# Which channels of a Haar inverse put their last convolution off: 27 instead of 23 of 64, two and three apart

## The chip, the cores and the metric

The kernel runs on one core of one Trainium2 chip. The metric is the device time of one execution in microseconds (us). Before the change the median of three runs is 2845.51 us (2843.74 to 2846.02). The engines are named as in the profile: PE (TensorE: matmul), DVE (VectorE), ACT (ScalarE), POOL (GpSimd) and SP (SyncE, which here only issues transfers).

## What is computed

The input x is 4 batches of 64 channels of 256 x 256, in float32. Four layers follow each other. Layers 0, 1 and 3 are separable long convolutions: each channel is convolved with the outer product of two filters, and gets a bias times itself added. Layer 2 is a Haar transform in two dimensions, then a mixing over the channels of each coefficient, and the inverse transform with x added:

```python
def _conv(x, ...):                       # layers 0, 1, 3, shortened
    k = einsum('ijk,imk->ijmk', hx, hy)  # one outer product per channel
    y = irfft2(rfft2(x, 2L) * rfft2(k, 2L))[..., :L, :L]
    return y + x * bias[:, None, None]

def _haar(x, v, conv_w, tau):            # layer 2
    f1 = haar2d(x)
    acc = 0
    for i in range(2):
        f4 = einsum('bchw,oc->bohw', f1 * v[i], conv_w[i])
        acc = acc + sign(f4) * relu(abs(f4) - tau[i])
    return haar2d(acc, inverse=True) + x
```

The convolutions of one channel don't depend on other channels; the mixing needs all 64 channels of a batch, and so does each channel of the inverse.

## The kernel before, in words

**A convolution** is two products with Toeplitz matrices of the two filters (`contract`, L283: four matmuls each, lines L286 and L287, each of which the profile shows twice[...]). The first product `pa` is copied out of PSUM by ACT (L300), the second, `py`, takes that copy, and DVE adds the bias term while it reads `py` from PSUM (L317). The Toeplitz tile `t` of a channel is loaded from a padded filter in HBM (L277, 256 KB, six buffers).

**The stages.** For each batch: `convolutions` (layers 0 and 1, and the Haar transform of the columns), `mixing` (64 groups of coefficients), `inverse` (64 channels). The convolutions of batch b + 1 are spread over the mixing of batch b, with a few at the edges. In the mixing, a group is loaded (`f`, L460), mixed by PE into `px` (L480), scaled partly by DVE (L502) and partly by ACT (L507, 8 columns in the last batch, 12 in the others), then ACT takes the size and the sign (L511, L514), and DVE subtracts the threshold, puts the sign back, and adds (L518, L522, L528). In the inverse of a channel, ACT gathers the coefficients (`zc`, L569), PE does the rows (`pw`, L576 and L577, called row matmuls below), the first 16 channels also need a column matmul (`pu`, L590), DVE joins the result with the saved part `r` (loaded at L558; L598, L601, L602) into `u`. Further halvings of columns (L326, L329) run on DVE during the first 38 channels. Then layer 3 follows for the channel: `pa`, its copy, `py`, its sum, and the store to the output from ACT's queue.

**Put-off channels.** In the inverses of batches 0 to 2 the channels in the list `put_off` (L673) do not run layer 3. Their `u` is stored to the HBM buffer `late` from SP's queue (`aside`, L606), their Toeplitz tile isn't loaded (`sooner`, L561). The last mixing has no convolutions of a next batch beside it; there `convolution` (L655) loads `u` back as the tile `v` (L662, three buffers), and the Toeplitz tile, runs layer 3 and stores to the output from SP's queue (L652).

**The order of the work.** Time is counted in ticks: one mixing group or one inverse channel is one tick. The table `PLACE` gives each step a place in ticks relative to its channel's or group's tick (for a put-off channel in the last mixing: load at +0.316, `pa` and its copy at +1.855, `py` and its sum at +2.783, store at +4.4). All steps are collected as events, sorted by that place (L723) and emitted in this order; the scheduling layer that records the program then sets the final order on each engine. Each engine works in order. `spread` (L669) lays n convolutions over a number of ticks, rounded down to whole ticks: the put-off ones over the 71 ticks from two before the last mixing to three before its inverse. In an inverse, a channel that is not put off is shifted a little within its tick (L644) unless both neighbours are put off: one pair of shifts for a channel that follows a put-off one, the other for a channel that stands before one.

Of the kernel before, what the change touches and what calls it, by code (L numbers as in the profile page):

```python
# [16 lines left out]
B, C, S, EMB, ORD = 4, 64, 256, 33, 64  # L17
# [93 lines left out]
def conv_seq_kernel(ctx, tc, x, fz, fw, bias, decay, haar, haar_row, factors, vt, taut, wmix, out):  # L111
# [236 lines left out]
    def at(time, run, unit):  # L348
        events.append((time, len(events), run, unit))
# [201 lines left out]
    def inverse(b, start, put_off):  # L551
# [78 lines left out]
        for c in range(C):  # L630
            for name, stage in zip(("sooner", "early", "fetch", "rows"), (sooner, early, fetch, rows)):
                at(start + c + PLACE[name], stage, c)
            turn = start + c
            if c < 16:
                at(start + c + PLACE["halves"], halves, c)
                at(start + c + PLACE["cols"], cols, c)
                turn += 1
            at(turn + PLACE["join"], join, c)
            if c in put_off:
                at(turn + PLACE["aside"], aside, c)  # L640
            else:
                shift = (0.0, 0.0)
                if put_off and not {c - 1, c + 1}.issubset(put_off):
                    shift = ((-0.27, -0.342), (0.23, 0.158))[c % 3]  # L644
                for name, stage in zip(("a3", "a3 copy", "y3", "y3 sum", "out"), last(b, st)):
                    at(turn + PLACE[name] + shift[name[0] != "a"], stage, c)

    def last(b, st, queue=nc.scalar):
        return [
            *first(b, st, "u", 2, "a3"),  # L650
            *second(b, st, "a3", 2, "u", "y3", "co"),
            lambda c: queue.dma_start(out[b, c].rearrange("(k p) w -> p k w", p=P), st.pop(c)["y3"]),  # L652
        ]
# [16 lines left out]
        return [begin + i * (end - begin - 1) // (n - 1) for i in range(n)]  # L670


    put_off = [*range(2, 53, 3), *range(53, C, 2)]  # L673

    clamped = {}, {}, {}
    one = filters(0, nc.scalar, clamped[0], None, clamped[1])
# [33 lines left out]
    for b in range(B):  # L710
        mixing(b, start, N_ACT[b])
        end = start + groups + 3
        if b + 1 < B:
            ready = convolutions(b + 1, spread(ahead, end + 2), in_parts=range(C), border=end)
        else:
            convolution(
                [(i, c) for i in range(B - 1) for c in sorted(put_off)], spread(start - 2, end + 2, (B - 1) * len(put_off))
            )
        inverse(b, end, put_off if b + 1 < B else ())

        start = max(end + C, ready + 3)
        ahead = start - 3
# [114 lines left out]
```

## Time and profile before

The profiled execution took 2842.56 us; its span, from the first to the last instruction, is 2840.7 us. The granted clock is 1.00 throughout.

| what | us | share of the span |
|---|---|---|
| PE busy | 2732.7 | 96% |
| DVE busy | 2494.6 | 88% |
| ACT busy | 2077.6 | 73% |
| POOL busy | 333.9 | 12% |

The stages, from the first `px` or `pw` of one to that of the next:

| stage | from, us | length, us | DMA, GB/s |
|---|---|---|---|
| convolutions of batch 0 | 20 | 415 | 236 |
| mixing 0 and convolutions of batch 1 | 435.4 | 420.1 | 209 |
| inverse 0, with 41 convolutions of layer 3 | 855.5 | 184.5 | 274 |
| mixing 1 and convolutions of batch 2 | 1040.0 | 458.5 | 209 |
| inverse 1, with 41 convolutions | 1498.5 | 184.5 | 275 |
| mixing 2 and convolutions of batch 3 | 1683.0 | 458.5 | 210 |
| inverse 2, with 41 convolutions | 2141.5 | 179.8 | 277 |
| mixing 3, with 69 put-off convolutions | 2321.3 | 289.4 | 244 |
| inverse 3, with 64 convolutions | 2610.7 | 230 | 221 |

The list of transfers gives, from issue to landing, a median of 4.1 us for `t` and for `r`, 3.5 for `f`, and 4.2 for the stores to the output from ACT's queue.

How to read it: a share of busy time over the whole span mixes stages that different engines bound, so each stage has to be looked at by itself. Records of one engine overlap (the next instruction starts before the record of the last ends), so an instruction's cost on a full engine is the distance between starts, not the length of its record. Idle time counts only on the engine that bounds its stage.

### The profile page before, as it was taken

How to read it: one execution, taken by the hardware profiler on the slowest of the kernel's cores; microseconds unless marked ns; L12 is line 12 of the kernel's file. 1: busy time of each engine (PE TensorE's matmuls, PEld its weight loads, DVE VectorE, ACT ScalarE, POOL GpSimd, SP SyncE). 2: the span in 40 equal slices, each digit the busy share in tenths (PEclk: the TensorE clock that was granted, in tenths of full speed). 3: DMA queues.
4: the chain of work that ended last, by engine and by line, in shares of the span. 5: the costliest groups of instructions: out<-in, count | busy, mean ns of one | idle time of the engine just before them, and what ended most of it. 6: DMA issues, size and time to landing. Idle time of an engine off the chain costs nothing. (4 is left out here: it accounts for less than half of the span.)

```text
span 2840.7 us, 56683 instructions
## 1 busy us (share of the span) xinstructions
PE 2732.7 (96%) x18642; PEld 2438.6 (86%) x18642; DVE 2494.6 (88%) x4333; ACT 2077.6 (73%) x4941; POOL 333.9 (12%) x644
## 2 busy tenths in 40 slices
PE   9999999999999999999999999999999999899999
PEld 8999998888889898888889998888889987787998
DVE  5655558999998979999998879999998889999985
ACT  2333348999986559989886658999985669998554
POOL 0111111121111001212210001312210000000000
PEclk9999999999999999999999999999999999999999
DMA  6877787676667886777677986777778988787786
GB/s 200 258 232 231 227 239 220 209 208 208 206 207 251 287 257 203 211 212 209 205 216 246 292 262 201 210 210 214 208 212 241 296 277 249 234 253 228 227 240 200
DMA packets 597209, 653.20 MB, mean 230 GB/s; under 512 B 44625, under 2 KB 513204, under 8 KB 596660
## 3 DMA queue, kind: packets, MB, share of 16 engines
q1 hardware_dynamic: 545460, 599.82, 70.6%
q10 hardware_dynamic: 51456, 49.75, 5.1%
q8 instruction: 150, 2.46, 0.4%
q14 instruction: 143, 1.17, 0.1%
HBM read 428.34 MB, written 221.05 MB: 229 GB/s over the span
## 5 line engine op out<-in xcount | busy, mean ns | idle before, releaser
L286 PE MATMUL py<-t,a 128*128 128x256 f32 x3072 | 946.3, 390 | 48.7 <-ACT a L300 47.7
L300 ACT COPY a<-pa 128x512 f32<-128x512 f32 x768 | 475.1, 619 | 476.6 <-PE pa L287 448.3
L507 ACT ACTIVATE f<-px,vt 128x64 f32<-128x64 f32 x2816 | 607.6, 354 | 104.2 <-DVE f L502 101.9
L287 PEld LDWEIGHTS py<-t,a 128*128 128x128 f32 x3072 | 583.4, 190 | 79.3
L287 PE MATMUL py<-t,a 128*128 128x128 f32 x3072 | 590.0, 274 | 0.0
L286 PEld LDWEIGHTS py<-t,a 128*128 128x128 f32 x3072 | 479.4, 191 | 112.2 <-ACT a L300 74.6
L380 POOL TENSOR_TENSOR sd<-less 128x128 f32<-128x128 f32 (+4 forms) x320 | 188.5, 589 | 1829.7 <-DVE less L379 1498.1
L286 PE MATMUL pa<-t,y 128*128 128x256 f32 x1024 | 316.5, 391 | 45.0 <-DVE y L317 44.2
L569 ACT COPY zc<-z 128x512 f32<-128x512 f32 x256 | 280.8, 1105 | 104.6 <-PE pw L577 96.7
L518 DVE TENSOR_TENSOR mag<-mag,vt 128x1024 f32<-128x1024 f32 x256 | 316.5, 1236 | 7.5 <-ACT mag L511 6.7
L522 DVE SCALAR_TENSOR_TENSOR mag<-mag,f 128x1024 f32<-128x1024 f32 x256 | 317.4, 1240 | 0.9 <-ACT f L514 0.5
L286 PE MATMUL pa<-t,x 128*128 128x256 f32 x1024 | 308.7, 383 | 0.6 <-DMA pad<-z 0.6
L403 DVE TENSOR_TENSOR sp<-sd,sp 128x512 fp32r<-128x512 f32 x256 | 179.3, 700 | 145.7 <-ACT sp L398 144.3
L480 PE MATMUL px<-wb,f 64*128 64x128 f32 x4096 | 303.7, 285 | 2.2 <-ACT f L507 2.2
L511 ACT ACTIVATE mag<-f 128x1024 f32<-128x1024 f32 x256 | 293.9, 1148 | 5.2 <-DVE z L528 1.2
L514 ACT ACTIVATE f<-f 128x1024 f32<-128x1024 f32 x256 | 283.9, 1109 | 4.1
L480 PEld LDWEIGHTS px<-wb,f 64*128 64x128 f32 x4096 | 252.2, 187 | 36.5 <-ACT f L507 3.0
L317 DVE SCALAR_TENSOR_TENSOR y<-x,bsb,py 128x512 f32<-128x512 f32 x256 | 190.3, 743 | 44.0 <-PE py L287 40.6
L286 PE MATMUL pa<-t,u 128*128 128x256 f32 x748 | 224.6, 382 | 0.7 <-PE pw L577 0.7
L287 PEld LDWEIGHTS pa<-t,y 128*128 128x128 f32 x1024 | 194.5, 190 | 26.4
L287 PEld LDWEIGHTS pa<-t,x 128*128 128x128 f32 x1024 | 194.6, 190 | 26.3
L286 PEld LDWEIGHTS pa<-t,y 128*128 128x128 f32 x1024 | 155.6, 191 | 65.3 <-DVE y L317 62.8
(71 smaller groups left out, 4434.6 us busy)
## 6 DMA issues: line engine op xcount, KB each, us to landing
t<-pad SPq DMA_DIRECT2D x767, 256.0 KB, 4.1
x<-in_x SPq DMA_DIRECT2D x256, 256.0 KB, 3.9
coef<-co SPq DMA_DIRECT2D x256, 256.0 KB, 3.2
f<-coef SPq DMA_DIRECT2D x256, 256.0 KB, 3.5
r<-keep SPq DMA_DIRECT2D x256, 256.0 KB, 4.1
out_y<-y ACTq DMA_DIRECT2D x187, 256.0 KB, 4.2
keep<-sums SPq DMA_DIRECT2D x256, 128.0 KB, 2.8
keep<-sd SPq DMA_DIRECT2D x256, 128.0 KB, 2.7
```

The source lines that it names most:

```text
L286: nc.tensor.matmul(ps[:, m, :], src[:, 0, m * P : (m + 1) * P], t[:, ::-1], start=True, stop=False)
L287: nc.tensor.matmul(ps[:, m, P:], src[:, 1, m * P : (m + 1) * P], t[:, : P - 1 : -1], start=False, stop=True)
L300: nc.scalar.copy(a, s["p" + new])
L317: nc.vector.scalar_tensor_tensor(y, s[res], bsb[:, layer, c : c + 1], s["p" + new], ALU.mult, ALU.add)
L380: engine.tensor_tensor(t[:, :, :, half:length], v[..., 0], v[..., 1], ALU.subtract)
L480: nc.tensor.matmul(ps[:, r, q, h * P : (h + 1) * P], f[half, q, h * P : (h + 1) * P], wb[half], start=True, stop=True,)
L507: nc.scalar.mul(f4[:, j], px[:, j // 4 % 2, j // 8, j % 4], scale(g, 0)[:, j : j + 1])
L511: nc.scalar.activation(mag, st[g]["f4"], AF.Abs)
L514: nc.scalar.activation(st[g]["f4"], st[g]["f4"], AF.Sign)
L518: nc.vector.tensor_sub(mag, mag, over(g, 1, 16))
L522: nc.vector.scalar_tensor_tensor(mag, mag, 0.0, st[g]["f4"], ALU.max, ALU.mult)
L569: nc.scalar.copy(a, v)
```

## The change

The list of put-off channels gets 27 members in place of 23. Before, it was every third channel from 2 to 50 and every second from 53 to 63. After, it is 2, 5, 7, 10, 12, 15 and so on up to 45, two and three apart in turn, then every second channel from 47 to 63. The three inverses keep 37 convolutions each in place of 41, and the last mixing gets 81 in place of 69. Since 81 is more than 71, `spread` puts two of them into one tick at ten of the ticks (the first of these, -2, 5 and 12, counted from the start of the last mixing, then every seventh up to 61); before, two of the ticks had none. The pair of shifts is now chosen by whether the next channel is put off, where before it was chosen by the channel's number modulo 3.

```diff
                 if put_off and not {c - 1, c + 1}.issubset(put_off):
-                    shift = ((-0.27, -0.342), (0.23, 0.158))[c % 3]
+                    shift = ((-0.27, -0.342), (0.23, 0.158))[c + 1 in put_off]
...
-    put_off = [*range(2, 53, 3), *range(53, C, 2)]
+    put_off = [c for c in range(46) if c % 5 in (0, 2) and c] + [*range(47, C, 2)]
```

## The prediction, made before the changed kernel was run

> **What bounds the kernel now.** I first read the busy time by stage (from the busy windows), because the change moves work from three stages into a fourth. The columns are the window and its length, then busy time and instruction count of each engine, the granted clock, the DMA share and GB/s.
>
> ```profile
> core 0: us, PE busy (x) PEld busy (x) DVE busy (x) ACT busy (x) POOL busy (x), PEclk, DMA share, GB/s
> 855.00:1040.00 185.00, 183.29 (x1200) 167.93 (x1198) 160.33 (x308) 111.12 (x145) 6.83 (x19) 1.00 0.86 274
> 1498.00:1683.00 185.00, 183.40 (x1200) 168.40 (x1198) 152.73 (x296) 112.67 (x147) 5.45 (x20) 1.00 0.87 275
> 2141.00:2321.00 180.00, 178.40 (x1167) 163.57 (x1167) 150.65 (x292) 111.15 (x145) 5.45 (x20) 1.00 0.89 277
> 1624.40:1680.00 55.60, 55.58 (x380) 51.98 (x379) 43.39 (x85) 32.04 (x38) 0.00 (x0) 1.00 0.93 290
> 2321.00:2600.00 279.00, 254.48 (x2051) 221.43 (x2050) 275.25 (x462) 265.49 (x694) 0.00 (x0) 1.00 0.81 245
> ```
>
> The first three rows are the inverses of batches 0 to 2: PE has work 99% of the time, DVE 83 to 87%, ACT 60%. The fourth is the last 24 ticks of one of them, where DMA reaches 0.93. The last row is the last mixing with the put-off channels in it: there DVE is full (99%), ACT 95%, PE 91%. So a channel that is put off leaves a stage that PE bounds and enters one that DVE bounds.
>
> Then I read the order of time on DVE and PE. DVE, at the end of the last mixing (start, us, line):
>
> ```profile
> 2595.89 1.34 DVE L518 TENSOR_TENSOR mag<-mag,vt 128x1024 f32<-128x1024 f32 x1
> 2597.02 0.88 DVE L528 TENSOR_TENSOR z<-mag 128x256 f32<-128x256 f32 x2
> 2597.69 1.35 DVE L522 SCALAR_TENSOR_TENSOR mag<-mag,f 128x1024 f32<-128x1024 f32 x1
> 2598.82 0.87 DVE L317 SCALAR_TENSOR_TENSOR y<-v,bsb,py 128x512 f32<-128x512 f32 x1
> 2599.48 0.88 DVE L502 TENSOR_TENSOR f<-px,vt 128x256 f32<-128x256 f32 x2
> 2600.14 1.35 DVE L518 TENSOR_TENSOR mag<-mag,vt 128x1024 f32<-128x1024 f32 x1
> ```
>
> A tick is the time from one L518 to the next: 2600.14 - 2595.89 = 4.25 us, with no idle time. Records overlap, so what an instruction costs is its distance to the next start: the put-off channel's sum (L317) costs 2599.48 - 2598.82 = 0.66 us, the rest of the tick 3.6.
>
> PE inside an inverse:
>
> ```profile
> 1585.00 0.38 PE L287 MATMUL pa<-t,u 128*128 128x128 f32 x2
> 1585.22 0.27 PE L577 MATMUL pw<-hrow,zc 128*128 128x128 f32 x1
> 1585.33 0.39 PE L576 MATMUL pw<-hrow,zc 128*128 128x128 f32 x2
> 1585.55 0.27 PE L577 MATMUL pw<-hrow,zc 128*128 128x128 f32 x1
> 1585.66 0.39 PE L576 MATMUL pw<-hrow,zc 128*128 128x128 f32 x2
> 1586.06 0.70 PE L286 MATMUL py<-t,a 128*128 128x256 f32 x2
> ...
> 1594.86 0.60 PE L286 MATMUL py<-t,a 128*128 128x256 f32 x2
> 1595.29 0.38 PE L287 MATMUL py<-t,a 128*128 128x128 f32 x2
> 1595.51 0.60 PE L286 MATMUL py<-t,a 128*128 128x256 f32 x2
> 1595.95 0.38 PE L287 MATMUL py<-t,a 128*128 128x128 f32 x2
> 1596.17 0.60 PE L286 MATMUL pa<-t,u 128*128 128x256 f32 x2
> ```
>
> Below the dots, one product takes 1596.17 - 1594.86 = 1.31 us of PE, so the two of a channel take 2.62. Above them is the price of a product that stands alone: only one channel's row matmuls (four, 0.66 us of slots) lie between pa and py, and the copy of pa on ACT doesn't fit: py starts at 1586.06 where 1585.88 would be possible, and its first matmul adds another 0.1; about 0.27 us are lost.
>
> **The change part by part.** The list goes from 23 to 27 channels, so four products' pairs leave each of three inverses (41 to 37) and 12 enter the last mixing (69 to 81). In the order of the built program all engines' orders are the same in the first three mixings and from the fifth channel of the last inverse on; only inverses 0 to 2 and the last mixing can move.
>
> *Removed from the inverses.* PE: 4 x 2.62 = 10.5 us each, 31.4 in all. It counts in full while PE is the bound. The ACT copies (0.57 us) and the DVE sums (0.66 to 0.75) that go with them lie beside PE. The store to out on ACT's queue becomes a store to late on SP's, of the same 256 KB; the load of the third layer's filters (256 KB) goes away. Behind the four more stores on SP stand the loads of r and t; the store stands after the sum of u at tick +2.36, where u is due at +1.43, so I price that at nothing; if u is late, SP stands still for that long, with the next r behind.
>
> *What is late next there.* (a) Lone products: by the built order, products with four row matmuls or fewer before py go from 6, 6 and 7 to 9, 11 and 12, so 13 more x 0.27 = 3.5 us; some of those of before lost nothing, so I take 2.4 (0 to 4). The changed choice of the shift (by the neighbour instead of c % 3) gives the same as before for the old list and moves nothing by itself. (b) DVE: in ticks 16 to 40 of inverse 0 the window 917.8 to 980.3 has DVE busy 61.12 of 62.5 us. There one channel more is put off (8 to 9): PE would save 2.6, DVE only 0.7 + 1.4 of idle time; 0.6 us are lost. Inverse 1 has 7.6 us less DVE work, inverse 2 no more than it, and I count no loss there. (c) DMA: in the last 24 ticks two more channels go (10 to 12), which would make 55.6 us into 50.4. Moved now: 55.6 x 290 GB/s = 16.1 MB, less two filter loads, 15.6 MB, is 309 GB/s; as a share, 0.93 x 55.6 = 51.7 us, less 2 x 0.84, is 50.0 of 50.4. The Trainium skill ("HBM Reference", Specifications) gives a core an effective 358 GB/s; by that there is room and the cost is nothing. By the row, 290 GB/s at 0.93 make the engines full at an estimated 312. I go with the row, but full is not yet late: 1 us an inverse, 3 in all (0 to 7).
>
> *Added to the last mixing.* 81 channels over 71 ticks: ten ticks take two channels (before, none did, and two were empty). DVE: 12 x 0.66 = 7.9 us, on the path. PE: a double tick asks for 4 products and the px matmuls, 4 x 1.31 + 1.0 = 6.2 us, and DVE then takes 4.25 + 0.66 = 4.9. The built order spreads it: py, pa, pa, px in one tick and py, py, pa, px in the next, 3 x 1.31 + 1.0 = 4.9 each. Over seven ticks with eight channels PE needs 28 us and DVE 30.4. px stands a whole tick ahead of L502 in the trace, so PE can be late by some us. ACT: 8 x L507 1.74 + 1.03 + 0.98 + 0.47 = 4.2 us a tick by distances, 4.7 in a double one. Loads: a put-off channel's v waits for a buffer of three:
>
> ```profile
> SPq L662 <- DVE y L317: 88.2, 57, 2.9
> ```
>
> SP waits there for the sum of three channels before, with the store to out and the next f load queued behind it. In the trace v is issued at 2462.84 and its product is three channels on, at about 2461.2 + 2 x 4.26 = 2469.7: 6.9 us of lead. In a double tick the second channel comes 4.26 - 1.31 sooner: 4.0 us of lead, against a landing of 3.2 (2.7 to 4.5). So a load can now be late by up to 0.5 us in a stage whose DMA share goes from 0.81 to about 0.89 (12 x 3 x 256 KB more on 68 MB, over 288 us). DVE's sum stands about 0.6 us after py's end in a single tick (2461.4 to 2462.02), which covers most of it. I take 1.5 us for all ten double ticks (0 to 8; nothing speaks for a gain).
>
> **Sum.** -31.4 + 2.4 + 0.6 + 3.0 + 7.9 + 1.5 = -16.0 us. The profiled execution took 2842.6 us (span 2840.7), so 2826.6; the median of the runs is 2.9 above it: 2829.5.
>
> One rule reads against this. The Trainium skill ("Perfetto Trace Analysis", Identifying the Most-Contended Engine) says to improve the engine with the highest occupancy. Over the whole span that is PE with 96%, and the change leaves PE the same products: by that the gain is nothing. By stage the same row splits into 99% where products leave and 91% where they enter; so I keep the stage sum.
>
> **The rivals.** *Clean*: no losses, -31.4 + 7.9 = -23.5, 2822. For it: PE never waits long in the trace; against it: the DMA share and the lone products. 17%. *The inverses hit DMA*: each keeps only a quarter of its 10.5, 3 x 2.6 = 7.9, against 7.9 + 1.5 in the mixing: 2847, no change. For it: 0.93 over 55 us and single stretches at 1.0; against: stretches of 8 us at 1.0 show no idle PE. 9%. *The double tick breaks the rhythm* (slower): the second channel's v is late by a whole landing of 3.2 us because its store and loads stand behind the wait on SP, PE stands in order before px, and DVE gets neither its sum nor L502. Price: 10 x 3.2 = 32 in place of the 1.5, which gives 2860. From 1.75 us lost per double tick on, the whole change is a loss; the lead of 4.0 us against 3.2 speaks against it. 9%. The likeliest, as summed: 65%.
>
> About 0.2% is what a measurement can tell: 2839.8 and 2851.2 are the bounds. Faster: clean and likeliest, with a little of the others: 83%. Same 9%, slower 8%. The range takes in clean with the least costs, 2820, and the likeliest with DMA and double ticks at their upper ends (-16 + 4 + 6.5, 2840).
>
> **What would show it.** Each inverse shorter by 8 to 10 us with PE still at 99% and DMA at 0.90 or more; the last mixing longer by 8 to 13 us with DVE at 99%, double ticks of 4.9 us, and no L317 waiting long for py. Wrong if PE's idle time in the inverses grows by over 3 us each, or if double ticks take 6 us or more.

## The result and the profile after

The changed kernel takes 2859.01 us (median of four runs, 2856.7 to 2861.1) against 2844.89 us (2843.74 to 2846.02) for the kernel before on the same chip: a ratio of 1.0049 (95% interval 1.0032 to 1.0067). It is slower by half a percent, where 2829.5 us were forecast. The profiled executions have spans of 2858.7 and 2840.7 us. By stage (from the first `px` or `pw` of one to that of the next), in us, with differences taken before rounding:

| stage | before | after | difference | forecast |
|---|---|---|---|---|
| mixings 0, 1 and 2 | 1337.1 | 1339.1 | +1.9 | 0 |
| inverses 0, 1 and 2 | 548.8 | 531.1 | -17.7 | -25.4 |
| last mixing | 289.4 | 320.0 | +30.6 | +9.4 |
| last inverse, to the last matmul | 226.2 | 228.9 | +2.7 | 0 |

These differences add to 17.5; another 0.5 us lie ahead of the first mixing. The 1.9 us lie in the two of the first mixings whose granted clock was 0.996 (421.4 and 459.2 us, against 420.1 and 458.5 at 1.00); the third, at 1.00, takes 458.5 in both kernels. So the inverses gave less than was forecast, and the last mixing took three times what was forecast.

The busy windows of the changed kernel for the first inverse and for the last mixing (window, length, busy time and count of PE, PEld, DVE, ACT and POOL, granted clock, DMA share, GB/s):

```profile
857.20:1036.40 179.20, 175.41 (x1131) 158.09 (x1129) 157.75 (x304) 109.12 (x141) 6.44 (x18) 1.00 0.89 276
2305.90:2625.90 320.00, 291.52 (x2266) 255.25 (x2266) 312.27 (x508) 281.56 (x719) 0.00 (x0) 1.00 0.85 247
```

In the inverses PE's share is lower than before (97.9% in the first, where it was 99%), though DVE and ACT have no more to do. In the last mixing DVE is still at 98%, so the added time isn't idle time: DVE was given 312.3 us of records, where its window of before has 275.3 in 279. Eleven more sums (L317) stand in it, which explains 7.3 of that; the twelfth fell into the last inverse. The order of time on DVE, around a double tick of the changed kernel, shows the rest:

```profile
2440.19 1.22 DVE L518 TENSOR_TENSOR mag<-mag,vt 128x1024 f32<-128x1024 f32 x1
2441.32 0.76 DVE L528 TENSOR_TENSOR z<-mag 128x256 f32<-128x256 f32 x2
2441.99 1.22 DVE L522 SCALAR_TENSOR_TENSOR mag<-mag,f 128x1024 f32<-128x1024 f32 x1
2443.13 1.22 DVE L326 TENSOR_TENSOR z<-z 128x1024 f32<-128x1024 f32 x1
2444.27 0.75 DVE L502 TENSOR_TENSOR f<-px,vt 128x256 f32<-128x256 f32 x2
2444.93 1.40 DVE L317 SCALAR_TENSOR_TENSOR y<-v,bsb,py 128x512 f32<-128x512 f32 x2
2446.24 1.22 DVE L518 TENSOR_TENSOR mag<-mag,vt 128x1024 f32<-128x1024 f32 x1
...
2449.19 1.22 DVE L329 SCALAR_TENSOR_TENSOR z<-z 128x1024 f32<-128x1024 f32 x1
...
2451.64 1.22 DVE L518 TENSOR_TENSOR mag<-mag,vt 128x1024 f32<-128x1024 f32 x1
```

A double tick is one that takes two put-off channels. This one, from L518 to L518, takes 2446.24 - 2440.19 = 6.05 us: the 4.92 that were forecast (two sums, 2444.93 to 2446.24) and 1.13 for an L326. The next tick takes 5.40: 4.26 and 1.13 for an L329. Those two are column halvings of batch 3, which belong to the last inverse. The groups of DVE in the last mixing, of the kernel before and then of the changed one (count | busy us, mean ns | idle before):

```profile
L326 DVE TENSOR_TENSOR z<-z 128x64 f32<-128x64 f32 (+4 forms) x10 | 5.0, 520 | 0.0
L329 DVE SCALAR_TENSOR_TENSOR z<-z 128x64 f32<-128x64 f32 (+4 forms) x10 | 5.0, 512 | 0.0
```

```profile
L326 DVE TENSOR_TENSOR z<-z 128x1024 f32<-128x1024 f32 (+4 forms) x20 | 14.6, 742 | 0.0
L329 DVE SCALAR_TENSOR_TENSOR z<-z 128x1024 f32<-128x1024 f32 (+4 forms) x20 | 14.7, 742 | 0.0
L317 DVE SCALAR_TENSOR_TENSOR y<-v,bsb,py 128x512 f32<-128x512 f32 x77 | 56.6, 742 | 5.0 <-PE py L287 4.8
```

By distances between starts, L326 and L329 together took 8.9 us in the last mixing before and take 26.7 now (+17.8). In the last inverse they fall from 48.1 to 30.0, which is no gain: PE bounds it, and DVE's idle time there grows from 35.9 to 53.2 us. In the last mixing the sums L317 add 7.4 us (44.2 to 51.6), idle time of DVE adds 5.3 (4.8 to 10.1). 17.8 + 7.4 + 5.3 = 30.5 of the 30.6.

Of the idle time, 4.8 us are sums that wait for `py` (above). That isn't a source apart from late `v` loads: where `v` is late, `pa` and then `py` are. The waits of the last mixing show one row for `v` (total us, times, longest), here with SP's own wait at the load:

```profile
PE pa L286 <- DMA v<-late: 4.6, 3, 1.8
```

```profile
SPq L662 <- DVE y L317: 54.8, 65, 2.3
```

SP still stands at the `v` load for the sum of three channels before, though the sum of these waits is smaller than before.

In the inverses the waits of the first one have new rows, PE's first product waiting for `u`. Before, then after:

```profile
PEld pa L286 <- DVE u L602: 0.2, 1, 0.2
```

```profile
PEld pa L286 <- DVE u L602: 3.2, 5, 0.9
PE pa L286 <- DVE u L602: 2.0, 5, 0.6
```

One of them in order of time, on DVE and then on PE:

```profile
933.33 0.69 DVE L326 TENSOR_TENSOR z<-z 128x512 f32<-128x512 f32 x1
...
934.60 0.68 DVE L329 SCALAR_TENSOR_TENSOR z<-z 128x512 f32<-128x512 f32 x1
...
937.07 0.42 DVE L602 TENSOR_TENSOR u<-t 128x256 f32<-128x256 f32 x1
```

```profile
937.55 0.70 PE L286 MATMUL pa<-t,u 128*128 128x256 f32 x2 [0.62 <-DVE u L602]
```

Two halvings, which cost 0.60 us each by distance, stand among the joins ahead of that `u`, and PE has nothing to do for 0.62 us. A lone product (a `py` with only one channel's row matmuls ahead of it) of the changed kernel, in inverse 1, waits as those of before did:

```profile
1539.63 0.70 PE L286 MATMUL py<-t,a 128*128 128x256 f32 x2 [0.27 <-ACT a L300]
```

PE's time in the inverses that its matmuls' usual distances don't account for, sorted by the matmul that came late, is in the three inverses: ahead of `pa` 0.9, 0.5 and 0.5 us before and 4.3, 2.3 and 2.3 after; ahead of `py` 2.1, 2.0 and 2.5 before and 3.2, 4.6 and 4.6 after; ahead of `pw` 2.3, 2.4 and 2.4 before and 3.2, 2.1 and 1.8 after.

### The profile page after: what moved, and what is told of

Read it like the earlier page. It is cut to its first block, busy times and chain, and to the rows that moved or that the text cites. A ratio compares the mean times of both kernels' runs of the same rounds, so it can differ in the third digit from the quotient of the medians.

```text
span 2858.7 us, 56729 instructions
## 1 busy us (share of the span) xinstructions
PE 2746.3 (96%) x18642; PEld 2443.0 (85%) x18642; DVE 2500.3 (87%) x4333; ACT 2081.7 (73%) x4941; POOL 325.4 (11%) x644
## 5 line engine op out<-in xcount | busy, mean ns | idle before, releaser
L507 ACT ACTIVATE f<-px,vt 128x64 f32<-128x64 f32 x2816 | 609.4, 354 | 120.0 <-DVE f L502 114.6
L518 DVE TENSOR_TENSOR mag<-mag,vt 128x1024 f32<-128x1024 f32 x256 | 312.1, 1219 | 6.8 <-ACT mag L511 5.7
L522 DVE SCALAR_TENSOR_TENSOR mag<-mag,f 128x1024 f32<-128x1024 f32 x256 | 313.0, 1223 | 1.1 <-ACT f L514 0.7
L480 PEld LDWEIGHTS px<-wb,f 64*128 64x128 f32 x4096 | 253.6, 188 | 34.2 <-issue 2.8
L317 DVE SCALAR_TENSOR_TENSOR y<-x,bsb,py 128x512 f32<-128x512 f32 x256 | 189.7, 741 | 44.0 <-PE py L287 40.0
L286 PE MATMUL pa<-t,u 128*128 128x256 f32 x700 | 211.5, 384 | 3.7 <-DVE u L602 2.7
L286 PEld LDWEIGHTS pa<-t,y 128*128 128x128 f32 x1024 | 156.1, 191 | 65.0 <-DVE y L317 62.5
```

The costliest lines, as they stand in the source:

```text
L286: nc.tensor.matmul(ps[:, m, :], src[:, 0, m * P : (m + 1) * P], t[:, ::-1], start=True, stop=False)
L317: nc.vector.scalar_tensor_tensor(y, s[res], bsb[:, layer, c : c + 1], s["p" + new], ALU.mult, ALU.add)
L480: nc.tensor.matmul(ps[:, r, q, h * P : (h + 1) * P], f[half, q, h * P : (h + 1) * P], wb[half], start=True, stop=True,)
L507: nc.scalar.mul(f4[:, j], px[:, j // 4 % 2, j // 8, j % 4], scale(g, 0)[:, j : j + 1])
L518: nc.vector.tensor_sub(mag, mag, over(g, 1, 16))
L522: nc.vector.scalar_tensor_tensor(mag, mag, 0.0, st[g]["f4"], ALU.max, ALU.mult)
```

## The experiments

Sixteen more kernels were run. Each ratio is to the kernel before as it ran beside that kernel on the same chip (medians from 2843.9 to 2845.4 us), so the times of different rows differ by up to 1.5 us for that reason alone. "Mixing" below is the time from the last row matmul of the third inverse to the first of the last one, since some of these kernels start the last mixing within the third inverse; the profiled kernels have 289.4 us before and 320.0 after by it. "Halvings" are L326 and L329 in that stretch, by distances; DVE's idle time is that of the stretch, which leaves out the 0.5 to 2 us around its first instructions that the sum above has.

| kernel | time, us | ratio to before (95%) | mixing | halvings | DVE idle | last inverse |
|---|---|---|---|---|---|---|
| before | 2844.89 | 1 | 289.4 | 8.8 | 4.3 | 226.2 |
| after | 2859.01 | 1.0049 (1.0032 to 1.0067) | 320.0 | 26.7 | 8.3 | 228.9 |
| before_bunched | 2863.76 | 1.0065 (1.0053 to 1.0078) | 309.6 | 25.8 | 4.3 | 222.2 |
| before_hold | 2846.18 | 1.0005 (0.9997 to 1.0013) | 290.0 | 5.5 | 7.4 | 226.7 |
| after_hold | 2872.61 | 1.0097 (1.0083 to 1.0111) | 326.2 | 5.6 | 31.7 | 235.5 |
| hold_even | 2876.88 | 1.0111 (1.0098 to 1.0125) | 331.3 | 5.6 | 34.2 | 234.5 |
| after_v5 | 2855.69 | 1.0038 (1.0026 to 1.0051) | 314.8 | 26.8 | 3.8 | 228.8 |
| hand | 2851.13 | 1.0020 (1.0012 to 1.0028) | 301.7 | 5.6 | 14.1 | 231.4 |
| before_hand | 2848.59 | 1.0012 (1.0005 to 1.0018) | 284.9 | 5.8 | 4.9 | 227.8 |
| hand2 | 2847.79 | 1.0011 (1.0002 to 1.0019) | 303.6 | 5.7 | 13.6 | 229.6 |
| hand2d | 2845.39 | 1.0005 (0.9997 to 1.0013) | 302.6 | 5.7 | 12.7 | 229.6 |
| hand2d_lone | 2844.28 | 0.9999 (0.9991 to 1.0007) | 304.3 | 5.9 | 12.8 | 229.6 |
| sum_a | 2849.14 | 1.0015 (1.0008 to 1.0021) | 305.5 | 5.4 | 12.3 | 229.6 |
| sum_b | 2849.98 | 1.0018 (1.0011 to 1.0025) | 306.1 | 5.5 | 12.6 | 229.6 |
| sum_c | 2845.91 | 1.0007 (0.9999 to 1.0015) | 302.4 | 5.7 | 12.3 | 229.6 |
| sum_d | 2845.01 | 1.0002 (0.9994 to 1.0010) | 307.6 | 5.7 | 15.1 | 223.6 |
| lists71 | 2845.53 | 1.0006 (0.9998 to 1.0014) | 293.0 | 8.4 | 6.4 | 229.7 |

The sixteenth, after_nolate, leaves out work and was run once: 2850.89 us.

### Where the halvings come from: before_bunched, before_hold, after_hold, hold_even

**before_bunched** leaves the list of before as it is, and lets its channels end nine ticks earlier: 69 channels in 62 ticks make some ticks double and leave the last ones without a channel:

```diff
-  spread(start - 2, end + 2, (B - 1) * len(put_off))
+  spread(start - 2, end - 7, (B - 1) * len(put_off))
```

> The kernel before with its 69 put-off channels spread over 62 ticks in place of 71, so that some seven ticks take two; no channel more is put off and the three inverses stay as they are. The built order then has 23.8 thousand elements per partition of halvings in the last mixing in place of 8.7. Theory 1: 14.7 lengths of 1.13 us more on full DVE, 16.7 us, so about 2862 us. Theory 2 (idle time of DVE at the double ticks alone, 0.5 us each): 2848 to 2850 us with the halvings filling what the ticks without a channel leave free at the end.

Measured: 2863.76 us, as the theory of the halvings had it, and not the 2848 to 2850 of the other. No channel was added, and 25.8 us of halvings stand in the mixing in place of 8.8: the 17.0 us are most of the mixing's 20.2. The group of L326 in its last mixing:

```profile
L326 DVE TENSOR_TENSOR z<-z 128x1024 f32<-128x1024 f32 (+4 forms) x21 | 15.0, 720 | 0.0
```

So the longer list isn't needed: spacing the channels into double ticks brings the halvings in. Nine of the fourteen longest (1.13 us each) stand in a double tick or the tick beside it; three stand in the last ticks, which have no channel here. That the time grew by 18 us with the inverses' work unchanged also shows that the mixing is where a gain is lost.

**before_hold** and **after_hold** keep the halvings of batch 3 behind the joins of the last inverse, in either kernel:

```diff
-  level(n, chunk, *span, stay=stay)
+  level(n, chunk, *span, stay=stay or b + 1 == B)
```

> The kernel before, with the same constraint on the halvings of batch 3 (8.7 thousand elements per partition in the last mixing become 4.2 thousand). Theory 1: 4.4 lengths of 1024 less on full DVE, 4.9 us, so about 2840 us. Theory 2: no change, 2845 us. A third possibility: the last inverse gets longer by what the mixing saves, 2845 us.

> The changed kernel, with the halvings of batch 3 kept behind the joins of the last inverse, so that fewer of them stand in the last mixing on DVE (4.2 thousand elements per partition in place of 25.7 thousand). Theory 1 (the halvings that moved out of the last inverse, where PE hid them, now lie on full DVE in the last mixing, 1.13 us for each of 1024 elements): 21 such lengths less, 23.7 us, so about 2835 us, and the last inverse no longer. Theory 2 (the double ticks break the rhythm, and the halvings only fill time in which DVE would stand idle): 2853 to 2859 us, with idle DVE in the last mixing in place of the halvings.

Measured: the kernel before doesn't change (2846.18 us). The changed one gets slower by 13.6 us, where theory 1 had a gain of 24 and theory 2 at most 6. It lies outside both. The halvings did go (5.6 us left), and the idle time of DVE took their place and more (8.3 to 31.7 us). The waits of its last mixing:

```profile
PE py L286 <- ACT a L300: 30.7, 39, 3.0
ACT f L507 <- DVE f L502: 17.4, 16, 2.1
DVE mag L518 <- ACT mag L511: 15.9, 33, 2.0
```

DVE, ACT and PE wait for each other in turn. Without the halvings the scheduling layer ordered DVE anew: in many ticks L502 stands behind L522 and the sums. ACT, which has 4.2 us of work in a tick of 4.26, then starts L507 late and doesn't catch up. That this order causes the waits is argued here; the orders written by hand below test it. So the halvings are what fills DVE in the changed kernel, but taking them out doesn't give their time back: the order that is left loses more. More products end up behind the mixing too (five first and six second ones in place of three and four), which makes the last inverse longer.

**hold_even** is after_hold with the 81 channels at even distances in fractions of a tick, so that no two have the same place:

```diff
-  return [begin + i * (end - begin - 1) // (n - 1) for i in range(n)]
+  return [begin + i * (end - begin - 1) // (n - 1) if n <= C else begin + i * (end - begin - 1) / (n - 1) for i in range(n)]
```

> The changed kernel with the halvings kept back, and the 81 put-off channels spread evenly over the 71 ticks, in fractions of a tick, so that no tick takes two at the same place. Theory 1: the bunching itself costs little, the idle time of DVE in the last mixing of the changed kernel is 10 us against 5 before, so 2 to 5 us under the run with the halvings kept back, about 2831 us. Theory 2: the bunching is the cost, so this run gains 15 us or more on that one.

Measured: 2876.88 us, 34.2 us of idle time. Even places don't help. They don't do away with double ticks either: in DVE's order, about every seventh tick from L518 to L518 still has two sums and takes about 7.6 us, with 1.4 of them idle. So this run doesn't tell what a mixing without double ticks would take; lists71 does.

### Late loads: after_v5

Five buffers instead of three for `v` (it shares those of `u`); nothing else:

```diff
-  u = io.tile([P, 2, S], F32, name=f"v_{b}_{c}", tag="in", bufs=3)
+  u = io.tile([P, 2, S], F32, name=f"v_{b}_{c}", tag="y", bufs=BUFS["y"])
```

> The changed kernel with one edit: the loads of the put-off u (tile v) rotate over the five buffers of u, which stand idle in the last mixing, in place of three, so that a load no longer waits for the sum of three channels before. Theory L (in a double tick v comes late, and on SP the stores and f loads stand behind its wait): the last mixing gets 5 to 10 us shorter, 2849 to 2854 us. Theory O (what is lost stems from the order on the engines at the double ticks, and from halvings that the scheduling layer puts there): no change, 2857 to 2861 us.

Measured: 2855.69 us, the mixing 5.2 us shorter, PE's wait for `v` gone from the list, and DVE's idle time 4.5 us less. The sums' wait for `py`, 4.8 us in the changed kernel, falls with it:

```profile
DVE y L317 <- PE py L287: 0.9, 2, 0.6
```

The time lies between the two expectations: late loads cost about 5 of the 30.6 us. The forecast had 1.5 for all that a double tick loses.

### An order written by hand: hand, before_hand, hand2, hand2d

**hand** holds the halvings, has the five buffers, gives the steps of the last mixing new places, and ties PE's, DVE's and ACT's instructions there to the order of these places (`tc.add_manual_dep` from each to the one before it on its engine). The order on DVE is that of the kernel before (L502, L518, L528, L522, L317). Of the places:

```diff
-    "l a3": 1.855,
+    "l a3": 0.5,
...
-    "l y3 sum": 2.783,
+    "l y3 sum": 1.7,
...
-    "l mix": 0.21,
+    "l mix": -1.1,
```

> The changed list of 27 channels, with the halvings of batch 3 kept in the last inverse, v over five buffers, and the order of PE, DVE and ACT in the last mixing written out and pinned: in every tick DVE does L502 of the group, L518, L528 and L522 of the ones before, then the channels' sums; ACT the copies of pa between halves of L507; PE py, pa, then px two groups ahead. Theory O: DVE then loses no time in double ticks; the last mixing is that of before plus 7.9 us for 12 sums less up to 4.9 us of halvings, 290 to 296 us, the inverses keep the 17.8 us that the changed kernel's trace shows, so 2826 to 2834 us. Rival I (a double tick can't be covered, whatever the order, since ACT with 4.7 us and DVE with 4.9 of a tick wait for each other): the last mixing stays above 312 us, 2850 us or more.

**before_hand** is the same edit on the kernel before.

> The kernel before with its 23 channels and the same three edits (halvings kept back, v over five buffers, pinned order). It has no double ticks. Theory O: the order of before was nearly this one already, so only the halvings count, 2840 to 2845 us, and the list of 27 under the same edits is 10 to 16 us faster than this run. Rival I: also 2840 to 2845 us, but the list of 27 under the same edits is slower than this run.

Measured: 2851.13 and 2848.59 us. From tick 9 on, every single tick of hand without a halving takes 4.26 us, and it has 14.1 us of idle time instead of after_hold's 31.7: it was mostly the order (with the early loads) that cost after_hold its time. Its later double ticks take 6.02 us, 0.90 of them idle, so its time is the rival's, not the 2826 to 2834 of the other. But its last mixing also starts among the last channels of the third inverse, which takes 180.6 us to its last row matmul where the changed kernel has 173.6. before_hand has the same loss (185.4 where before has 179.6), gains 4.5 us in the mixing and loses 1.6 in the last inverse; it misses the 2840 to 2845 of both expectations.

**hand2** is hand with all of its places one tick later. **hand2d** also puts the second sum of a double tick 0.55 ticks later, behind the next L502 and L518, and its transfer behind it.

> The written order of the last mixing again (81 channels, halvings of the fourth batch held behind its joins, v loads with five buffers), all of its places one tick later than in the first try, and nothing else changed. Theory S (start): the first try lost about 12 us in ticks 0 to 8, because its products and sums came 1.4 ticks early and stood among the last channels of the third inverse; its double ticks of 6.02 us against single ones of 4.26 are the only other loss. Then the last mixing falls from 311.4 to 297 to 302 us and the kernel takes 2837 to 2842 us, faster than before. Theory W (no slack): with ScalarE at 4.2 of 4.26 us and VectorE full, any written order pays a start of its own, and the time stays at 2848 to 2853 us.

> As the kernel ahead of it, but in a double tick the second channel's sum stands behind the next tick's first scaling and subtraction on VectorE (0.55 ticks later), and its output transfer behind it. Theory S: the double tick's wait of 0.9 us for the second product (VectorE, sum waiting for py) goes, double ticks fall from 6.0 to about 5.0 us, and the kernel is 7 to 10 us below the one ahead of it. Rival: the wait only moves to another place in the same round (the PSUM buffer of the sum is held longer, so TensorE starts the next product later, or ScalarE has no gap to make up), and the two kernels are within 3 us.

Measured: 2847.79 and 2845.39 us. hand2 was to be 2837 to 2842: the third inverse is 4.0 us shorter than in hand, the rest of the 12 us that I ascribed to the start was never lost, since hand's first `px` stands 9.5 us ahead of the third inverse's last row matmul and I had counted from there. hand2d was to gain 7 to 10 us on hand2 by its double ticks, and the rival held: the mixing is 1.0 us shorter. Two lines of hand2d, a double tick's two waits for `py`:

```profile
2467.85 0.75 DVE L317 SCALAR_TENSOR_TENSOR y<-v,bsb,py 128x512 f32<-128x512 f32 x1 [0.73 <-PE py L287]
...
2473.06 0.75 DVE L317 SCALAR_TENSOR_TENSOR y<-v,bsb,py 128x512 f32<-128x512 f32 x1 [0.21 <-PE py L287]
```

In hand2 this was one wait of 0.94 us (a double tick of 6.04 and a single one of 4.26 behind it); here it is 0.73 and 0.21, the two ticks 5.08 and 5.22. The pair costs 1.78 us more than two single ticks in both, where 0.66 were forecast.

### The price of a double tick: sum_a, sum_b, sum_c, sum_d

**sum_a** puts every sum behind the next L502, **sum_b** one instruction later still, **sum_c** only the sums of double ticks; **sum_d** is sum_c with the 81 channels ending three ticks earlier (`end - 1`).

> The written order with the halvings held, as hand2d, but every channel's sum stands behind the next tick's L502 on VectorE (0.66 us later), and the second one of a double tick behind that tick's L518 too. Theory of the order: a double tick costs 1.78 us over a single one (0.66 forecast) only because its sums stand where TensorE has just finished py; with 0.66 us of slack VectorE never waits there, double ticks cost 0.7 to 0.9 us more than single ones, and the kernel takes 2834 to 2838 us, faster than before by 0.25 to 0.4%. Theory of TensorE: a double tick and the tick behind it ask for six products and two px groups beyond what two ticks of VectorE give (2 x 4.93 = 9.9 us against 9.2), whatever stands where; the wait moves to the next product or to px, the pair of ticks stays at 10.2 to 10.3 us, and the kernel takes 2842 to 2847 us.

> As sum_a, with the sums one instruction later still (behind L518, the second one behind L528). Theory of the order: no wait for py is left at all, and the time is that of sum_a or up to 2 us below it, 2833 to 2838 us. Theory of TensorE: the PSUM buffers are held 1.1 us longer than in sum_a, the products wait for them, and the time is that of sum_a or longer, 2843 to 2852 us.

> As hand2d, but only the two sums of a double tick get slack: the first stands behind the next L502, the second behind the next L518; in single ticks the sum stays between L522 and L502. In sum_a all ticks had the sum behind L502; its double ticks fell to 5.11 us, and every single tick rose from 4.26 to 4.46, with 0.2 us between L522 and an L502 that stood right behind it. If that is the whole account, single ticks are 4.26 again and double ticks 5.1 us, with 0.2 us more in the tick that loses its sum: ten double ticks give 7 to 9 us to hand2d, 2836 to 2839 us, faster than before by 0.2 to 0.3%. Rival: TensorE's six products in two ticks put the wait back into the tick behind (a single tick of 4.9 to 5.1 us behind each double one), and the time stays at 2843 to 2847 us.

> As sum_c, with the 81 channels ending three ticks earlier (68 ticks, 13 double ones), so that the last of their products leave the last inverse, which TensorE bounds. Account: two to three channels' products of 2.62 us leave the inverse (229.6 to 222 to 225 us), and three more double ticks add 3 x 0.85 = 2.6 us to the mixing: 3 to 5 us below sum_c, 2832 to 2835 us. Rival: denser double ticks (every fifth in place of every seventh) leave TensorE or ScalarE no time to recover, the mixing grows by as much as the inverse loses or more, and the time is that of sum_c or longer.

Measured: 2849.14, 2849.98, 2845.91 and 2845.01 us; none of them has the gain that was looked for. In sum_a double ticks fall to 5.11 us, 0.65 over the single ones, but every single tick is 4.46 instead of 4.26, since L502 then starts 1.32 us after L522 where L317 starts 1.14 after it. With ticks that long the sums of sum_a don't wait for `py` (no wait of DVE from 2400 to 2600 us). With single ticks of 4.26 (sum_c) the wait comes back in the tick behind the double one:

```profile
2475.59 0.75 DVE L317 SCALAR_TENSOR_TENSOR y<-v,bsb,py 128x512 f32<-128x512 f32 x1 [0.81 <-PE py L287]
```

The pair is then 4.45 + 5.81 = 10.26 us, against hand2d's 10.30. So in a written order with single ticks of 4.26 us a double tick costs the mixing about 1.75 us wherever its sum stands, and it is `py` on PE that is late; what keeps PE from being ahead (its `py` waits for ACT's copy in two ticks of three) wasn't tried apart. sum_d shows the other end: the last inverse is 6.0 us shorter with the last products out of it, and the mixing 5.2 us longer. It comes to the same.

### The inverses: after_nolate, hand2d_lone

**after_nolate** is the changed kernel without the late halvings (ticks 18 to 38) of the first three inverses.

```diff
-                        for j in range(2):
+                        for j in range(0):
```

> The changed kernel without the late halvings (L326 and L329 in ticks 18 to 38) of the inverses of batches 0 to 2: that part of the inverse transform is left out, so its time is that of less work. Theory D (u comes late from DVE, since its halvings stand before the joins, and pa waits on PE): the time that PE loses ahead of pa in these inverses, 4.3, 2.3 and 2.3 us, falls to under 0.7 each, and the inverses get 1.5 to 3.5 us shorter. Rival (loads of r or of the filters come late): no shorter.

Measured: the inverses take 174.2, 175.4 and 172.7 us instead of 179.2, 178.0 and 173.8 (8.7 us less in all), and PE's loss ahead of `pa` falls from 4.3, 2.3 and 2.3 to 0.8, 0.7 and 0.8. DMA moves the same bytes there. So `u` was late because of DVE, not because of transfers. The 8.7 us are not the 6.6 of `pa` alone: by a count of the same kind PE's loss ahead of `pw` falls too, by about 5, and its loss ahead of `py` grows by about 3.5. The inverses got 5.0, 2.6 and 1.1 us shorter, where 1.5 to 3.5 each were expected.

**hand2d_lone** is hand2d with the second product of a channel that stands alone ordered behind the next channel's row matmuls.

> As the kernel ahead of it, but in the first three inverses a channel that stands alone between two put-off ones has its second product ordered behind the next channel's row products on TensorE, and its sum 0.55 ticks later. Theory (lone products): most of what the added channels failed to save in the inverses is the second product standing 0.3 to 0.5 us on ScalarE's copy; with another channel's row products ahead of it TensorE's loss before the second products falls from 3.2, 4.6 and 4.6 us to below 2 each, and the three inverses are 6 to 9 us shorter in all. Rival: the copy is late because ScalarE is late, not because TensorE had nothing else, or the held PSUM bank makes the next first product wait: the inverses change by less than 3 us in all, or get longer.

Measured: PE's loss ahead of `py` falls from 3.2, 4.2 and 4.3 (hand2d) to 2.1, 2.7 and 2.8, and ahead of `pw` it rises from 3.3, 1.8 and 2.1 to 4.6, 3.9 and 3.6. The inverses take 178.6, 178.3 and 170.1 us against 179.2, 177.3 and 169.6: nothing is gained. The rival held; the loss is moved from the product to the row matmuls.

### A smaller step: lists71

24, 24 and 23 channels, 71 products in 71 ticks, none double:

```diff
-    put_off = [c for c in range(46) if c % 5 in (0, 2) and c] + [*range(47, C, 2)]
+    put_off = [*range(2, 48, 3), *range(49, C, 2)]
...
+    [(i, c) for i in range(B - 1) for c in put_off[: 24 - i // 2]], spread(start - 2, end + 2, 71)
...
+    inverse(b, end, put_off[: 24 - b // 2] if b + 1 < B else ())
```

> 24, 24 and 23 put-off channels (every third up to 47, then every second), so 71 products in 71 ticks of the last mixing, one to a tick and none double; everything else as changed, no written order. If the double ticks are what lets the halvings in (theory T), the last mixing has about 9600 elements of halvings as built and takes 290 to 293 us (289.4 before), and the first two inverses are 1.5 to 2.6 us shorter each: 2841 to 2844 us, the same as before or just faster. If instead any fuller last mixing loses by its number of channels alone (a third of the loss per added channel: 2.5 us each), it takes 294 us or more and the kernel 2846 to 2849 us.

Measured: the halvings stay out of the mixing (8.4 us), as the theory of the double ticks had it, and the first two inverses are 2.1 and 1.8 us shorter. The kernel is no faster than before (1.0006), and above the 2841 to 2844 that this theory had, because the mixing is 3.6 and the last inverse 3.5 us longer. The part of the last inverse I had not counted: it holds 24 and 32 matmuls of put-off channels' first and second products where it held 16 and 24 before, one whole channel more, 2 x 1.31 = 2.6 us on PE. The changed kernel has the same 24 and 32, which is its +2.7 us.

## Why the prediction was wrong

**What bounds each stage** was right: PE in the inverses, DVE in the last mixing. So was the direction of the large terms.

**The step that failed first** is the sentence that all engines' orders "are the same in the first three mixings and from the fifth channel of the last inverse on; only inverses 0 to 2 and the last mixing can move". For the last inverse that holds for neither DVE nor PE: ten more L326 and ten more L329, 17.8 us of work, had left the last inverse for the last mixing, and one put-off channel's products had gone the other way (+2.7). Both stand in the order of the built program. In the last inverse the halvings were free, as DVE is idle there for 36 us or more; in the mixing, where DVE is full, they take their whole length. before_bunched (double ticks without a longer list: 25.8 us of halvings) and lists71 (a longer list without double ticks: 8.4) show that it is the double ticks that bring them in.

**Added to the last mixing.** The sums were right (7.9 forecast, 7.4 measured). The double ticks were priced at 1.5 us (0 to 8) and cost 23.1: 17.8 of halvings and 5.3 of idle time, most of it late `v` loads (after_v5: 5.2). The 17.8 us are what the halvings occupy, not what the mixing would gain without them: from after_v5 to hand2d, which holds them back and has a written order, 21.1 us of halvings go, but DVE's idle time grows by 8.9 and the mixing is only 12.2 us shorter. While a halving runs on DVE, PE has time for a double tick's products (the later double ticks of after_v5 have no idle time); without it the sums wait for `py` (0.73 and 0.21 us in hand2d). So the prediction's own condition for a loss, 1.75 us lost per double tick, was met: with ten of them, it was 2.3. The rival *The double tick breaks the rhythm* had the right place and sign, but that its 2860 us are near the 2859.0 is luck: late loads cost 5 us where it had 32.

**"What is late next there", in the inverses.** 31.4 us left PE, 17.7 were gained, so 13.7 were lost where 6.0 were forecast. (a) Lone products: 2.4 forecast, 5.8 measured (12.4 us ahead of `py` in place of 6.6). (b) DVE: 0.6 forecast, 7.0 measured (8.9 us ahead of `pa` in place of 1.9). The argument compared busy time over a window of 62.5 us, where DVE would have had room left on average; but one join waits behind one halving of 0.6 us, and with fewer products in between PE has no other work while it does. (c) DMA: 3.0 forecast, nothing found: in the waits of the three inverses no row has PE waiting for a transfer. The last ticks of inverse 1 of the changed kernel, PE alone (window, length, PE busy, granted clock, DMA share, GB/s):

```profile
1619.50:1671.00 51.50, 51.43 (x349) 1.00 0.96 304
```

By this row full is an estimated 304 / 0.96 = 317 GB/s, near the prediction's 312, but full was not late; the 358 GB/s of the Trainium skill ("HBM Reference", Specifications) gave the better price here. The 304 GB/s lie below both figures, so no run shows which of them is a limit. 0.9 us remain unexplained.

**The sum.** With the halvings held, the loads early and the order written out, the mixing's price is 302.6 - 289.4 = 13.2 us (hand2d), not far from the 9.4. Even then the kernel only equals the one before: its inverses, to the last row matmul of the third, are 16.1 us shorter than before, its last inverse is 3.4 longer, and nothing is left. So two things were wrong independently: what the scheduling layer moved, and how much of PE's 2.62 us per channel the inverses give back (17.7 / 12 = 1.5).

**What stays open.** Why the scheduling layer lets the halvings pass in a kernel with double ticks was not tried; only that it does. How much of the 30.6 us the halvings cost net of what they cover has no run of its own, since hand2d also changes the order. Nor was it tried what a written order would need so that PE is ahead of DVE's sums at 4.26 us a tick. No kernel here beats the one before by more than can be measured.

## What to carry to other kernels

When a change moves work into a stage whose engine is full, look in the built order at everything on that engine, not only at what the diff names: here work that had been free in a neighbouring stage, under another engine's bound, came along and took more than twice the time that the change itself added (17.8 against 7.4 us). Count what each stage holds before and after, and count an order by its own time: taking the unwanted work out left an order that idled for as long. And an engine at 98% that waits for nothing for long still says nothing about whether its work belongs in that stage.

## What the runs showed of the hardware

**The granted clock.** A stage at 0.996 isn't a slightly slower stage. In these traces the clock is 1.00 but for short stretches at 0.50, most of them 3.41 us long; one of them in a mixing of 420 us makes the mean 0.996. One of the changed kernel:

```profile
587.10:590.40 3.30, 3.30 (x16) 2.67 (x15) 2.19 (x5) 1.86 (x3) 0.00 (x0) 0.50 0.49 159
```

Up to the end of the last mixing the eighteen traces have 27 such stretches, and each starts within 1.4 us of the end of an idle time of PE of 1.4 us or more; the one above follows 1.71 us in which PE waited for L317. The same wait stands in the kernel before (1.71 us, up to 585.76), and the clock stayed at 1.00 there, so such an idle time doesn't always bring it. Mixing 0, which no kernel changes, takes 420.0 to 420.6 us where its clock was 1.000 and 420.9 to 422.0 where it was 0.996. Where a difference is 2 to 3 us, that is much of it, so stage times are worth comparing only with the clock beside them. The longest stretch is in before_bunched, 20.5 us at the end of the mixing (0.97 over the mixing). PE has 4.5 us of work in it while DVE is full, so it can explain little of that kernel's loss. In after_hold's mixing three of 3.41 us stand behind waits of PE; at half clock they cost PE an estimated 3 x 1.7 = 5 us at most.

**A wait of DVE for itself.** In sum_a an L502 starts 1.32 us after the L522 ahead of it, where an L317 or L326 starts 1.14 after it; one such pair in each of 63 ticks is 12 us. The order of the two isn't the reason by itself: in after_hold and in the earlier mixings an L502 behind L522 mostly starts after 1.14 us. In sum_a most of these L502 wait for the semaphore that L522 signals, and DVE is idle for 0.10 us. What they share wasn't tried.
